# Layer 3's q and k products of both halves of a sample put side by side, and a gate convolution on 128 columns

## The chip, the cores and the metric

The kernel runs on one core of a Trainium2 chip. A core has five engines that run beside each other and meet through semaphores: TensorE (PE, the matrix products; its weight loads are listed as PEld), VectorE (DVE), ScalarE (ACT), GpSimd (POOL) and SyncE (SP, which here issues the transfers). Matrix products write to PSUM, of which this kernel keeps eight banks; the other operands lie in SBUF. The metric is the device time of one execution in microseconds (us): the median of three runs.

## The reference

Four layers are applied in turn to x of 16 samples, 256 channels and 32 x 32 pixels (1024 tokens), in 32-bit floats:

```python
# layer 0: attention of the pixels over one another
xn = group_norm(x, gamma, beta)                 # 8 groups
q, k, v = split(W_qkv xn + b_qkv)
x = x + W_proj(softmax(q k^T / sqrt(256)) v) + b_proj
# layer 1: a gate from two planes of the image
w1, w2 = mean(x, channels), max(x, channels)
w3 = relu(conv3x3([w1, w2]) + b1)
x = x * sigmoid(conv3x3(w1 + w2 + w3) + b2)
# layer 2: attention as in layer 0, with its own norm and weights
# layer 3: attention with 32 channels for q and k, and clipped energies
energy = clip((Wq x + bq)^T (Wk x + bk) / sqrt(32), -10, 10)
x = gamma * (Wv x + bv) softmax(energy)^T + x
```

## The kernel before, in words

The samples are worked on in two streams, called lanes: even samples in one, odd ones in the other. Each lane is a Python generator (`stream`), and one step of it ends at a `yield`; the kernel takes a step of each lane in turn, after a head start of 30 steps (`OFFSET`) for the even lane. The steps and the pauses between them (the `W_` numbers; `wait(n)` gives n empty steps) thus set which work of one sample stands beside which work of the other. A framework then fixes the order of the instructions of each engine when the program is built.

A large matrix product is made with seven block products in the place of eight (`seven`): it takes combined blocks of its left operand (`combine`, L900 to L905, tile xs) and of its right operand, and adds the seven results up in four PSUM banks. The banks' letters are the names in the profile: b, a, c and f, with a prefix. Products of the first attentions' q and k side are tb, ta, tc, tf; of the values (`values`) vb, va, vc, vf, evicted into the tile vt; of the logits (`logits`) sb, sa, sc, sf, evicted into e by ACT copies (L672) and DVE additions (L603), with exponentials on ACT (L682, L684). In `seven` a bank is read by ACT's copy between two products that add into it: sb<-tc must be copied before the next product, sb<-t, adds to the same bank.

`weighted` (L687) makes the product of the exponentials and the values in the same way, on banks b, af and c. Its steps are b(vt), af(tv), af(vt), c(tv), b(tv), c(vt), b(vt), named here by the operand in brackets. DVE makes the combined operands cb (L698) and further ones in e (L699, L746, L751). After c(tv), DVE takes a reciprocal of the row sums (L755) and ACT copies the bank (L756), and then c(vt) adds into it; after c(vt) come L762, additions (L725) and the update of the tokens (L732). All these products are recorded by one helper (`product`, L571), so the profile tells them apart by tile.

`group_norm` (L106) normalizes a sample that comes up: statistics on DVE (L114 to L134), a power on POOL (L138), coefficients on DVE (L141 to L144), and the scaling of one half on DVE (L145) and one on ACT (L146).

`clipped_attend` (L1053) is layer 3. For each half h of the tokens it makes q and k with eight products on 64 columns of the array (L1072: two row-halves of a bank side by side, two channel chunks, four pairs); three ACT evictions (L1084) and three DVE evictions (L1088) lay the bank out in the tile t_qk. After the evictions of the second half, DVE makes the combined blocks (`combine`). The first step of the values stands between the two halves. Then the values go on, and for each half of the queries and each half of the keys a block of eight score products (L1107, tile s, 32 rows of the array), four exponentials on ACT (L1123) and clips on DVE (L1128) follow, then `weighted`.

`gate_of` (L159) is layer 1. Its first convolution is two products (L169) of which only 32 columns of the array are used, with 32-column weights `k.toep[:, i, :]`, and its result stands in 32 partitions of a bank. Its second convolution (L182) uses weights of 128 columns, four copies of one 32-column matrix. `toep` holds six 32-column matrices: two of the first convolution and the four copies.

In the profile a 32-bit product appears as two instructions: a block of eight score products as 16, a group of eight products of `weighted` as 16. Where the same tile name serves several shapes, the timeline tells the shapes.

Of the kernel before, what the change touches and what calls it, by code (L numbers as in the profile page):

```python
# [16 lines left out]
P = 128  # L17
# [5 lines left out]
NH = HW // HALF  # L23
TPH = HALF // P
GROUP = 32
DQK = 32
G4 = P // DQK
PH = P // 2
STRIP = 32
# [122 lines left out]
def neighbours(nc, rows):  # L152

    own, before, after = (rows[i * STRIP : (i + 1) * STRIP] for i in range(3))
    nc.vector.tensor_copy(before[..., 1:], own[..., :-1])
    nc.scalar.copy(after[..., :-1], own[..., 1:])


def gate_of(nc, k, small, psum, ptag, pl, rows, nm):  # L159

    for g in range(NG):
        copy = nc.scalar.copy if g % 2 else nc.vector.tensor_copy
        copy(rows[:STRIP, :2, g * NT : (g + 1) * NT], pl[g * STRIP : (g + 1) * STRIP])
    neighbours(nc, rows[:, :2])
    c1 = psum.tile([P, HALF], FP, tag=ptag, name=f"c1_{nm}")
    for i in range(2):
        nc.tensor.matmul(  # L169
            c1[:STRIP, :STRIP], k.toep[:, i, :], rows[:, i, :], start=(i == 0), stop=(i == 1)  # L170
        )
    r1 = small.tile([STRIP, STRIP], FP, tag="r1", name=f"r1_{nm}")
    nc.vector.tensor_scalar(
        r1, c1[:STRIP, :STRIP], k.sc[:STRIP, S_B1 : S_B1 + 1], 0.0, ALU.add, ALU.max
    )
    yield None
    inner = rows[:STRIP, 2, :]
    nc.vector.tensor_tensor(inner, rows[:STRIP, 0, :], rows[:STRIP, 1, :], ALU.add)
    nc.vector.tensor_tensor(inner, inner, r1, ALU.add)
    neighbours(nc, rows[:, 2])  # L180
    c2 = psum.tile([P, HALF], FP, tag=ptag, name=f"c2_{nm}")
    nc.tensor.matmul(  # L182
        c2[:, :STRIP],
        k.toep[:, 2:, :].rearrange("p g j -> p (g j)"),
        rows[:, 2, :],
        start=True,
        stop=True,
    )
    yield None

    sg = small.tile([P, NT], FP, tag="sg", name=f"sg_{nm}")
    for g in range(NG):
        gs = slice(g * STRIP, (g + 1) * STRIP)
        nc.scalar.activation(
            sg[gs], c2[gs, g * NT : (g + 1) * NT], AF.Exp, bias=k.neg_b2[gs], scale=-1.0
        )
    nc.vector.tensor_scalar(sg, sg, 1.0, None, ALU.add)
    nc.vector.reciprocal(sg, sg)
    yield sg


def fast_path(nc, tc, k, bad, x, w_l0, w_l2, w_l3, qk_bias, v_bias, tap_idx, out):
# [7 lines left out]
    with ExitStack() as ctx:  # L210
# [16 lines left out]
        def bank(nm):  # L227
            return ps_m.tile([P, HALF], FP, tag="m", name=nm)
# [5 lines left out]
        def slot(what, lane, shape, nm):  # L234

            return qkvp.tile(shape, FP, tag=f"{what}_{lane}", name=f"{what}_{nm}", bufs=1)
# [304 lines left out]
        rows = [wts.tile([P, 3, STRIP], FP, name=f"rows{lane}") for lane in range(2)]  # L541
# [240 lines left out]
        def wait(steps):  # L782

            for _ in range(steps):
                yield
# [95 lines left out]
        def right_of(w, sums):  # L881

            return factors(
                [[w[:, kk, j * P : (j + 1) * P] for j in range(CC)] for kk in range(CC)],
                {
                    "t1": sums[:, 0],
                    "t2": sums[:, 1],
                    "t3": w[:, 0, P:],
                    "-t4": sums[:, 2],
                },  # L890
            )

        def left_of(xt, xs):


            blocks = [[xt[:, half(h), c] for c in range(CC)] for h in range(NH)]
            s1, s2, s4 = (xs[:, i] for i in range(3))
            return factors(blocks, {"s1": s1, "s2": s2, "s3": blocks[1][0], "s4": s4})
# [154 lines left out]
        def clipped_attend(xt, y, lane, b):  # L1053

            qk = slot("t", lane, [P, NH, 2, 2 * P], f"qk3_{b}")
            groups = ((1, 0, 0), (0, 1, 1), (0, 0, 0), (1, 1, 0))  # L1060
            vt = vts[lane]
            left = left_of(xt, slot("xs", lane, [P, 3, TPH, P], f"l3_{b}"))
            steps = values(lane, left, right_of(*folded["l3"]), f"l3_{b}")
            qt = TPH // 2
            for h in range(NH):
                ps = bank(f"qk3_{b}_{h}")


                for c in range(CC):
                    for i in reversed(range(2)):  # L1070
                        g0 = h * TPH + i * qt
                        nc.tensor.matmul(  # L1072
                            ps[i * PH : (i + 1) * PH, : qt * P].rearrange(
                                "p (g n) -> p g n", g=qt
                            ),
                            w3qk[:, c, i],
                            xt[:, g0 : g0 + qt, c],
                            start=(c == 0),
                            stop=(c == CC - 1),
                        )  # L1080
                low, high, full = slice(0, PH), slice(PH, P), slice(0, 2 * P)
                g0, g1, g2, g3 = (slice(g * DQK, (g + 1) * DQK) for g in range(G4))
                for to, src, blk in ((low, low, 0), (g2, g0, 0), (g2, g1, 1)):
                    nc.scalar.activation(  # L1084
                        qk[to, h, blk], ps[src, full], AF.Identity, bias=qb[src]
                    )
                for to, src, blk in ((low, high, 1), (g3, g3, 0), (g3, g2, 1)):
                    nc.vector.tensor_scalar(qk[to, h, blk], ps[src, full], qb[src], None, ALU.add)  # L1088

                if h:  # L1090
                    combine(left)
                yield
                if not h:
                    next(steps)
                    yield
            yield from steps
            tv = value_sums(lane)
            yield
            ri = small.tile([P, NT], FP, tag="ri", name=f"ri3_{b}")
            for h in range(NH):  # L1100
                e = expp.tile([P, NT, HALF], FP, tag="e", name=f"e3_{b}_{h}")
                for mh in range(NH):
                    ss = [bank(f"s3_{b}_{h}_{mh}_{g}") for g in range(G4)]
                    for j in range(2):
                        for g, (_, _, blk) in enumerate(groups):
                            gs = slice(g * DQK, (g + 1) * DQK)
                            nc.tensor.matmul(  # L1107
                                ss[g][:, j * 2 * P : (j + 1) * 2 * P].rearrange(
                                    "p (t g j) -> p t g j", t=TPH, g=2
                                ),  # L1110
                                qk[gs, mh, 1 - blk, j * P : (j + 1) * P],
                                qk[gs, h, blk].rearrange("p (g t j) -> p t g j", g=2, t=TPH),
                                start=True,
                                stop=True,
                            )

                    for a in range(2):
                        m = mh * TPH + 2 * a
                        part = e[:, m : m + 2, :]
                        by_strip = part.rearrange("p m (t g n) -> p m t g n", t=TPH, g=2)  # L1120
                        for g, (ka, qa, _) in enumerate(groups):
                            if ka == a:
                                nc.scalar.activation(  # L1123
                                    by_strip[:, :, :, qa],
                                    ss[g].rearrange("p (m t n) -> p m t n", m=2, t=TPH),
                                    AF.Exp,
                                )
                        nc.vector.tensor_scalar(part, part, EXP_MIN, EXP_MAX, ALU.max, ALU.min)  # L1128
                    yield from wait(W_EXP)
                yield from wait(W_AV3)  # L1130
                if b == B - 1 and h == NH - 1:
                    last = combp.tile([P, TPH, C], FP, tag="cb", name="last")
                    yield from weighted(e, vt, tv, y, ri, h, f"l3_{b}", last)
                    store_last(last, b, h)
                    continue
                yield from weighted(e, vt, tv, y, ri, h, f"l3_{b}")
                turn_strips(y, half(h))
                chores[lane].extend(in_pairs(y, half(h), bstrip3))
                chores[lane].append(functools.partial(store_tokens, y, b, h))
                yield  # L1140
            count(ri, f"l3_{b}")
# [59 lines left out]
        ps = bank("badp")  # L1201
# [317 lines left out]
```

## Time and profile before

| what | number |
|---|---|
| runs (us) | 2702.98, 2702.78, 2701.82; median 2702.78 |
| profiled execution, span (us) | 2702.3 |
| mean granted TensorE clock | 0.997 of full speed |
| busy PE / PEld / DVE / ACT / POOL (us) | 2658.2 / 2366.0 / 2153.9 / 1327.9 / 45.4 |
| q and k products of layer 3 (L1072) | 256 instructions on 64 columns, 379 ns each |
| products of the first convolution (L169) | 64 instructions on 32 columns, 196 ns each |
| weight loads: 128, 64 and 32 columns (median) | 191, 136 and 110 ns |
| traffic | 123.07 MB moved, 46 GB/s |

The span is the time from the first to the last instruction of one profiled execution; its own time was not taken apart from it, and the median of the unprofiled runs lies 0.5 us above the span. PE's products are pipelined: an instruction's own duration (275 ns for one of 128 columns moved) is longer than the distance to the next one's start (112 ns in a dense row), so work on PE is counted by starts here: 112 ns for 128 columns moved, about 215 for 256 and 429 for 512. An arrow in a row, `out<-in`, names the tile written and those read; the brackets at the end name the idle time of the engine before the row and who ended it.

### The profile page before, as it was taken

Reading aid. Unit: us, or ns where it says so; the run is one execution under the profiler, and the core shown is the slowest. Engines: PE = TensorE matmul, PEld = TensorE weight load, DVE = VectorE, ACT = ScalarE, POOL = GpSimd, SP = SyncE. Lnnn points to the kernel's source line nnn. Section 1 sums busy time; section 2 is a strip of 40 time slices with the busy share of each in tenths; the row PEclk is TensorE's granted clock in tenths of the full one; section 3 lists DMA queues with packets and bytes.
Section 4 is the critical chain, followed back from the end, with each engine's and each line's share of the span. In section 5 each row is a group of like instructions: output and inputs, shape, how many; then the busy total and the mean of one; then the engine's idle time right before and its main releaser. Section 6 shows DMA issues by size and latency. Waiting matters only on the chain.

```text
span 2702.3 us, 47717 instructions
## 1 busy us (share of the span) xinstructions
PE 2658.2 (98%) x18998; PEld 2366.0 (88%) x18998; DVE 2153.9 (80%) x4242; ACT 1327.9 (49%) x2810; POOL 45.4 (2%) x118
## 2 busy tenths in 40 slices
PE   8999999999999999999999999999999999999997
PEld 6888988888988889889889898988989889898897
DVE  7988886888778887788867888678887788868776
ACT  3454455544455445544455544554454544545443
POOL 1000000000000000000000000000000000000000
PEclk9999999999999999999999999999999999999999
DMA  4021111212111120211201212112111121101111
GB/s 115 1 63 48 56 32 24 63 48 63 25 46 50 42 76 9 55 48 48 63 16 48 63 35 61 32 32 63 48 48 32 32 63 55 40 17 34 52 34 41
DMA packets 134823, 123.07 MB, mean 46 GB/s; under 512 B 10689, under 2 KB 125633, under 8 KB 134593
## 3 DMA queue, kind: packets, MB, share of 16 engines
q1 hardware_dynamic: 132720, 118.63, 15.7%
q8 instruction: 152, 2.49, 0.4%
q10 hardware_dynamic: 1872, 1.31, 0.2%
q14 instruction: 79, 0.64, 0.1%
HBM read 69.58 MB, written 50.33 MB: 44 GB/s over the span
## 4 chain that ended last, share of the span: by engine, by line
PE 81%; DVE 13%; ACT 4%; issue 2%; DMA 1%; POOL 0%; DVEq 0%; SPq 0%; ACTq 0%
PE b_l L571 15%; PE c_l L571 11%; PE af_l L571 11%; PE sb_l L571 10%; PE sc_l L571 8%; PE sf_l L571 4%; PE sa_l L571 3%; PE vb_l L571 3%; PE tb_l L571 3%; PE vc_l L571 2%; PE tc_l L571 2%; PE s L1107 2%; DVE e_l L603 1%; DVE vt L603 1%; PE vf_l L571 1%
## 5 line engine op out<-in xcount | busy, mean ns | idle before, releaser
L672 ACT COPY e_l<-sb_l 128x512 f32<-128x512 f32 x384 | 222.5, 584 | 217.9 <-PE sb_l L571 216.7
L571 PE MATMUL sb_l<-t_l,x 128*128 128x256 f32 x1024 | 262.0, 386 | 0.3
L571 PE MATMUL b_l<-vt,e_l 128*128 128x128 f32 x2048 | 251.8, 275 | 0.0
L571 PEld LDWEIGHTS b_l<-vt,e_l 128*128 128x128 f32 x2048 | 244.2, 192 | 5.4 <-issue 2.3
L571 PEld LDWEIGHTS sb_l<-t_l,x 128*128 128x128 f32 x1024 | 180.5, 191 | 40.1 <-ACT e_l L672 11.2
L682 ACT ACTIVATE e_l<-e_l 128x512 f32<-128x512 f32 x256 | 160.9, 630 | 86.6 <-DVE e_l L603 85.7
L684 ACT ACTIVATE e_l<-e_l 128x1024 f32<-128x1024 f32 x128 | 135.5, 1059 | 118.4 <-DVE e_l L603 118.4
L571 PE MATMUL c_l<-tv,cb_l 128*128 128x129 f32 x1536 | 189.0, 275 | 0.2 <-DVE cb_l L698 0.2
L571 PEld LDWEIGHTS c_l<-tv,cb_l 128*128 128x128 f32 x1536 | 180.3, 191 | 6.9 <-PE qk L1072 3.1
L603 DVE TENSOR_TENSOR e_l<-sc_l,e_l 128x512 f32<-128x512 f32 x128 | 88.0, 687 | 116.6 <-PE sc_l L571 114.9
L925 ACT COPY vt<-vb_l 128x512 f32<-128x512 f32 x144 | 84.5, 587 | 147.2 <-PE vb_l L571 146.1
L487 ACT ACTIVATE xr<-xr,bstrip 128x128 f32<-128x128 f32 (+1 forms) x376 | 134.4, 443 | 44.1 <-DVE xr L494 44.1
L1123 ACT ACTIVATE e<-s 128x512 f32<-128x512 f32 x256 | 131.8, 606 | 22.1 <-PE s L1107 21.4
L756 ACT COPY acc_l<-c_l 128x256 f32<-128x256 f32 x96 | 35.4, 368 | 212.3 <-DVE ri_l L755 151.8
L571 PE MATMUL sc_l<-tc_l,xs_l 128*128 128x256 f32 x512 | 134.0, 384 | 2.3 <-DVE vt L603 2.3
L571 PE MATMUL af_l<-tv,e_l 128*128 128x128 f32 x1024 | 131.6, 278 | 4.3 <-ACT e_l L682 4.3
L571 PE MATMUL sc_l<-t_l,xs_l 128*128 128x256 f32 x512 | 133.0, 382 | 0.8
L571 PE MATMUL sa_l<-t_l,x 128*128 128x256 f32 x512 | 132.4, 381 | 0.0
L571 PE MATMUL sf_l<-tc_l,x 128*128 128x256 f32 x512 | 131.7, 380 | 0.0
L571 PE MATMUL sb_l<-tc_l,xs_l 128*128 128x256 f32 x512 | 131.7, 379 | 0.0
L571 PEld LDWEIGHTS af_l<-tv,e_l 128*128 128x128 f32 x1024 | 121.3, 192 | 10.8 <-ACT e_l L682 7.7
L1128 DVE TENSOR_SCALAR e<-e 128x1024 f32<-128x1024 f32 x128 | 83.0, 687 | 59.0 <-ACT e L1123 59.0
(245 smaller groups left out, 5984.6 us busy)
## 6 DMA issues: line engine op xcount, KB each, us to landing
x<-mid_x SPq DMA_DIRECT2D x64, 512.0 KB, 3.3
xr<-in_x_dram SPq DMA_DIRECT2D x64, 256.0 KB, 4.9
mid_x<-t_z SPq DMA_DIRECT2D x128, 128.0 KB, 2.3
mid_x<-t_l SPq DMA_DIRECT2D x128, 128.0 KB, 2.3
x<-in_x_dram SPq DMA_DIRECT2D x62, 256.0 KB, 4.0
out_dram<-xr SPq DMA_DIRECT2D x124, 128.0 KB, 2.3
raw_l<-in_w_l_dram SPq DMA_DIRECT2D x1, 1024.0 KB, 6.9
raw_l<-in_w_l_dram SPq DMA_DIRECT2D x2, 256.0 KB, 5.5
```

The costliest lines, as they stand in the source:

```text
L487: nc.scalar.activation(y[:, s, ts], y[:, s, ts], AF.Identity, bias=bias[:, s : s + 1])
L571: mm = nc.tensor.matmul(out, left, right, start=fresh and m == 0 and (lone or i == 0), stop=(m == len(pairs) - 1), skip_group_check=True,)
L603: nc.vector.tensor_tensor(dst, src, dst, ALU.add)
L672: nc.scalar.copy(block(i, j), ps.rearrange("p (m n) -> p m n", m=2))
L682: nc.scalar.activation(part, part, AF.Exp)
L684: nc.scalar.activation(e[:, m : m + 2, :], e[:, m : m + 2, :], AF.Exp)
L756: nc.scalar.copy(acc[:, hi, c2], c[:, :, :P])
L925: nc.scalar.copy(block(i, j), ps.rearrange("p (m n) -> p m n", m=TPH))
L1107: nc.tensor.matmul(ss[g][:, j * 2 * P : (j + 1) * 2 * P].rearrange("p (t g j) -> p t g j", t=TPH, g=2), qk[gs, mh, 1 - blk, j * P : (j + 1 ...
L1123: nc.scalar.activation(by_strip[:, :, :, qa], ss[g].rearrange("p (m t n) -> p m t n", m=2, t=TPH), AF.Exp,)
L1128: nc.vector.tensor_scalar(part, part, EXP_MIN, EXP_MAX, ALU.max, ALU.min)
```

## The change

In `gate_of` the first convolution loads 128 columns of weights that begin at its 32-column matrix (the next three matrices ride along) and writes all 128 partitions of its bank. Of the result the same 32 partitions are read as before. In `clipped_attend` the first step of the values goes first and has a `yield` behind it; then the products of both halves follow directly on each other, the second half's first, without a `yield` between them; then the evictions of the first half, `combine`, and the evictions of the second half; then a `yield`. Before there were three yields up to this point, now there are two, so each later step of layer 3 of a sample comes one step earlier beside the other lane.

```diff
@@ gate_of
     c1 = psum.tile([P, HALF], FP, tag=ptag, name=f"c1_{nm}")
+    wide = k.toep.rearrange("p g j -> p (g j)")
     for i in range(2):
         nc.tensor.matmul(
-            c1[:STRIP, :STRIP], k.toep[:, i, :], rows[:, i, :], start=(i == 0), stop=(i == 1)
+            c1[:, :STRIP],
+            wide[:, i * STRIP : i * STRIP + P],
+            rows[:, i, :],
+            start=(i == 0),
+            stop=(i == 1),
         )
@@ clipped_attend
             qt = TPH // 2
-            for h in range(NH):
-                ps = bank(f"qk3_{b}_{h}")
-
-
+            next(steps)
+            yield
+            pss = [bank(f"qk3_{b}_{h}") for h in range(NH)]
+            for h, ps in reversed(list(enumerate(pss))):
                 for c in range(CC):
                     for i in reversed(range(2)):
                         g0 = h * TPH + i * qt
...
-                low, high, full = slice(0, PH), slice(PH, P), slice(0, 2 * P)
-                g0, g1, g2, g3 = (slice(g * DQK, (g + 1) * DQK) for g in range(G4))
+            low, high, full = slice(0, PH), slice(PH, P), slice(0, 2 * P)
+            g0, g1, g2, g3 = (slice(g * DQK, (g + 1) * DQK) for g in range(G4))
+            for h, ps in enumerate(pss):
                 for to, src, blk in ((low, low, 0), (g2, g0, 0), (g2, g1, 1)):
                     nc.scalar.activation(
                         qk[to, h, blk], ps[src, full], AF.Identity, bias=qb[src]
                     )
                 for to, src, blk in ((low, high, 1), (g3, g3, 0), (g3, g2, 1)):
                     nc.vector.tensor_scalar(qk[to, h, blk], ps[src, full], qb[src], None, ALU.add)
-
-                if h:
+                if h == 0:
                     combine(left)
-                yield
-                if not h:
-                    next(steps)
-                    yield
+            yield
             yield from steps
```

## The prediction

> **What bounds the kernel now.** I read the page's busy shares and chain first: TensorE (PE) is busy 98% of the span, and the chain that ended last is 81% PE. So a microsecond counts only where PE stands still or runs slowly. Then the waits of PE, longest first in total: they name every place where it stands.
>
> ```profile
> PE 2658.2 (98%) x18998; PEld 2366.0 (88%) x18998; DVE 2153.9 (80%) x4242; ACT 1327.9 (49%) x2810; POOL 45.4 (2%) x118
> ...
> PE 81%; DVE 13%; ACT 4%; issue 2%; DMA 1%; POOL 0%; DVEq 0%; SPq 0%; ACTq 0%
> ```
>
> ```profile
> PE af_l L571 <- ACT e_l L682: 4.3, 16, 0.3
> ...
> PE c_l L571 <- ACT acc_l L756: 2.4, 9, 0.3
> ...
> PE vc_l L571 <- DVE xs_l L902: 2.3, 1, 2.3
> ```
>
> The waits after set-up are a few tenths each, so there is little to win by removing them; but a step moved in PE's fixed order can make new ones. Both columns of the last three lines (times, longest) are used below. The body repeats every 330 us, one even and one odd sample per period (seven alike, and the last pair different); I work on the period of samples 8 and 9. Last come the timelines of PE, ScalarE (ACT) and VectorE (DVE) at the four places that the change moves. Columns: start, duration, engine, line, work.
>
> **1. The merge of the q and k products.** PE's timeline around one of the 32 blocks of eight products on 64 columns:
>
> ```profile
> 1652.12 1.95 PE L571 MATMUL b_l<-vt,e 128*128 128x128 f32 x16
> 1654.00 1.08 PE L1072 MATMUL qk<-x,w3qk 128*64 128x256 f32 x8
> 1655.01 1.12 PE L571 MATMUL tb_l<-x,m_l 128*128 128x512 f32 x2
> 1655.97 1.02 PE L571 MATMUL ta_l<-x,m_l 128*128 128x512 f32 x2
> ```
>
> The 16 products before take 16 x 0.112 = 1.79 us start to start, so the block's turn begins at 1653.91; the products after start at 1655.01, and the first pair of them needs 1655.97 - 1655.01 = 0.96 instead of 2 x 0.429 = 0.86, thus 0.10 of refill. Together 1.20 us. The eight products run in four pairs, two side by side, one pair each 0.215 us (the pace of a 256-wide product): 0.86. So going in and out of the 64-column form costs about 0.35. The change makes 16 blocks of 32: **-0.35 per sample, 16 x -0.35 = -5.6 us**, all of it on PE and uncovered. If the first pair of the second half were not overlapped this would shrink; bounds 0.25 to 0.45 per sample.
>
> A rule of the Trainium skill bears on it, "TensorEngine Tiling (Array Packing)", Key Properties: a change of tiling mode drains the array. The 0.35 above is the trace's price for it; the page has none.
>
> **2. The gate's first convolution.** 16 blocks of four instructions. An even sample's block stands between two parts of one product, PE's rows:
>
> ```profile
> 2441.02 0.61 PE L571 MATMUL af_l<-tv,e_l 128*128 128x128 f32 x4
> ...
> 2441.56 0.31 PE L169 MATMUL c_l<-rows,toep 128*32 128x32 f32 x4
> ...
> 2442.17 1.49 PE L571 MATMUL af_l<-tv,e_l 128*128 128x128 f32 x11 [0.30 <-ACT e_l L682]
> ```
>
> Its turn starts at 2441.02 + 4 x 0.112 = 2441.47, and the next product at 2442.17 (plus 0.10 refill): 0.80. But the last bracket says that PE then waited for ACT's e (the wait list counts it 16 times, 4.3 us). So a shorter block is paid back by that wait: worth 0. The odd block (2488.26) stands free and costs 0.44. In the full-width form the nearest row is the second convolution, L182, whose instructions start 0.103 to 0.112 apart: 4 x 0.107 = 0.43. **Change 0** for both; bounds -0.3 (the 128-wide steps overlap as the 32-wide do) to +0.3 (not even the loads hide) per gate, +-5 us over all, with 0 the likely value as both forms' rows agree.
>
> A rule speaks against this edit: "TensorE: Matmul & The Clock Gate", LDWEIGHTS, has a weight load cost its columns divided by 1.2 in nanoseconds. By it 128 columns for 32 are an estimate of 80 ns more per load, 64 loads, +5.1 us. The load records (110 ns for 32 columns, 191 for 128) show that step of 81 too, but PE's spacing does not follow them: 128-wide loads lie under 0.112 spacing everywhere. By the rows 0, by the rule +5.
>
> **3. What moves.** The value products' first step now goes ahead, one yield per sample is gone, and with it all later layer-3 work of a lane stands one step earlier among the other lane's work. Instruction counts of PE, DVE and ACT are unchanged, and the orders on the DMA queue (SP) and POOL too. The built program lists the new order; two stretches of it put a product nearer to what it waits for.
>
> *Wait A, even samples.* Before, the exps of the second score block (s, L1107) have two products of the other lane's logits behind them. Now the sequence on PE is s block, sb(tc), sc(t), third sb; on ACT the four exps of that s block, then the copy of sb(tc), on which the third sb (it adds into the same bank) waits. The durations come from the block at 1600.74:
>
> ```profile
> 1600.74 1.15 PE L1107 MATMUL s<-t_qk 32*128 32x256 f32 x16
> 1601.81 1.13 PE L571 MATMUL sc_l<-tc_l,xs_l 128*128 128x256 f32 x4
> 1601.96 2.07 ACT L1123 ACTIVATE e<-s 128x512 f32<-128x512 f32 x4 [1.34 <-PE s L1107]
> ...
> 1603.89 0.62 ACT L672 COPY e_l<-sc_l 128x512 f32<-128x512 f32 x1
> ```
>
> Call the s block's start S. The copy behind the exps ends at 1603.89 + 0.62 - 1600.74 = S + 3.77, and PE goes on 0.06 later: S + 3.83. PE is ready sooner: the next product starts at S + 1.07, has 0.10 of refill, and two groups of 0.865 stand before the third sb: S + 2.90. Wait 0.93, plus 0.10 refill: **+1.0 us**. Queued behind the stopped sb on PE is everything; behind the copy on ACT is only the copy that follows. In return the small waits of the old order (sc 0.16 at 1604.56, c and the s block 0.08) go: -0.24.
>
> *Wait B, even samples.* c(vt) adds into a bank that ACT's copy (L756) must first read; the copy needs DVE's reciprocal, and on ACT it stands behind the next sample's normalization (L146). Before, it was just in time:
>
> ```profile
> 1621.28 1.23 DVE L698 TENSOR_TENSOR cb_l<-e_l 128x1024 f32<-128x1024 f32 x1
> ...
> 1635.08 0.81 DVE L145 TENSOR_SCALAR x<-x,a_l,bb_l 128x1024 f32<-128x1024 f32 x1
> ```
>
> ```profile
> 1635.86 1.25 ACT L146 ACTIVATE x<-x,bb_l,a_l 128x1024 f32<-128x1024 f32 x1
> 1637.21 0.37 ACT L756 COPY acc_l<-c_l 128x256 f32<-128x256 f32 x1
> ```
>
> ```profile
> 1637.63 2.05 PE L571 MATMUL c_l<-vt,e_l 128*128 128x129 f32 x16
> ```
>
> From the end of the third sb (1619.07) to c(vt) PE had 18.6 us of work. In the new order one group of 16 products (1.79, the first c of sample 8) stands ahead of that sb and no longer between the two: 16.8. DVE's chain is not shorter. It starts with cb 2.2 after that sb, and from cb to the norm's coefficients took 1635.08 - 1621.28 = 13.8; in the new order the pause of 0.8 for POOL's power (DVE's idle before 1634.49) is filled by two clips of 0.6 each, and a reciprocal goes ahead too, so 14.2 to 14.4. Then ACT: norm 1.25, copy 0.37. Sum 2.2 + 14.3 + 1.25 + 0.37 + 0.05 = 18.2, against 16.8: **+1.3 us**, with refill about 1.4. It hides behind nothing. Bounds: 0 if the norm's chain starts earlier (DVE has 20% idle), 2.0 if the clips wait for exps. In the last pair there is no next sample to normalize, so no wait B.
>
> *Odd samples.* The logits' sc waits for DVE's vt at 1679.78 with 0.49 + 0.11; one step less cover makes it 0.8: +0.2. *Last pair.* The 2.3 us of vc for xs shrink, since the merge brings the combine on DVE nearer: about -1.2, beside A's +1.0 and the other gains: -0.8 in all.
>
> **Sum.** Per period: -0.70 merge, -0.24, +1.0 A, +1.4 B, +0.2 = **+1.66**; seven: +11.6; last pair -0.8: +10.8. From the profiled span of 2702.3: 2713.1; the median of the runs (2702.78) lies 0.5 above the span: **2714 us, +0.4%**.
>
> **Rivals.** R1: neither wait comes, since the shifted DVE and ACT work is early (for it: DVE is 20% idle, ACT 51%; against: both chains above are serial, with hardly an idle stretch): 16 x (-0.35 - 0.12), -7.5: 2695. R2: only one of A and B is there: A alone +0.26 a period, +1; B alone +0.66, +4: 2701 to 2707, no change to be measured. R3: B grows past 2 us and PE falls to half pace. The trace has one such case, and these rows (stretch, length, PE, PEld, DVE, ACT, POOL, granted clock, DMA) are before and after its 2.28 us pause:
>
> ```profile
> 2640.00:2647.00 7.00, 7.00 (x61) 5.77 (x59) 4.81 (x12) 2.80 (x7) 0.20 (x1) 1.00 0.28 90
> ...
> 2649.40:2652.90 3.50, 3.48 (x19) 3.48 (x20) 3.42 (x6) 1.50 (x3) 0.00 (x0) 0.59 0.57 150
> ```
>
> The clock fell to 0.59 for 3 us, about 1.6 us lost; pauses of 1.2 to 1.9 us at 2661 to 2682 show none. With B at 2.2 and this loss each time: 7 x (0.8 + 1.6) = +17 more, 2730. "TensorE: Matmul & The Clock Gate", Part 1, has the fall come after an idle window of some 3.4 us; here it came after 2.28. By the page R3 needs a longer wait. R4: the gate edit does not do what it says but costs 0.3 each: +5, inside the range.
>
> **Chances.** Both waits (forecast) 0.45; R1 0.13; R2 0.27; R3 0.10; others 0.05. The range 2695 to 2727 reaches R1's time and most of R3. What this kernel's measurement can tell from no change is 0.2%, 5.4 us. Faster (below 2697.4) 0.13; same 0.32 (R2, and the forecast with B at its low bound); slower 0.55.
>
> **What would show it.** In the profile after: 16 blocks of 16 qk instructions, each 0.35 shorter than two old ones; a wait of sb on ACT's copy of about 0.9, 8 times; a wait of c on L756's copy of about 1.3, 7 times; gate blocks at 0.43 (odd) with the af wait longer. I am wrong if the sb and c waits stay at tenths, or if waits turn up elsewhere, above all at s blocks or vb.

## The result, and the profile after

The changed kernel takes 2719.89 us in the median (2718.99 to 2723.19), against 2702.78 (2700.66 to 2703.83) before, five runs each: ratio 1.0062 [1.0051, 1.0073], 17.1 us slower. Here and below the brackets behind a ratio are its 95% interval. The forecast was 2714 in a range of 2695 to 2727: the side and the range were right, the size was short by 6 us. The profiled execution has a span of 2718.1 us (2702.3 before) and a mean granted clock of 0.996 (0.997).

Below, in this order: busy time by engine and the chain that ended last, both from the page after.

```profile
PE 2657.7 (98%) x18998; PEld 2373.3 (87%) x18998; DVE 2151.6 (79%) x4242; ACT 1329.4 (49%) x2810; POOL 55.3 (2%) x118
...
PE 75%; DVE 17%; ACT 5%; issue 2%; DMA 1%; POOL 1%; DVEq 0%; SPq 0%; ACTq 0%
```

The work is the same (the same counts, PE busy 0.5 us less), and the span grew by 15.8: PE stands still more. In the chain 6% of the span went from PE to DVE, ACT and POOL, so there are places where PE now waits for other engines. The waits of PE after name them (us in total, times, longest):

```profile
PE c_l L576 <- ACT acc_l L761: 12.6, 15, 1.9
...
PE sb_l L576 <- ACT e_l L677: 5.7, 9, 0.7
...
PE af_l L576 <- ACT e_l L687: 3.3, 16, 0.2
...
PE vc_l L576 <- DVE xs_l L907: 0.6, 1, 0.6
```

Lines of `product`, `logits` and `weighted` are 5 higher than before (L571 is L576, L756 is L761). The wait of c for ACT's copy rose from 2.4 to 12.6, and that of sb is new: waits B and A of the prediction, where it put them. The wait of vc for xs fell from 2.3 to 0.6.

**The merge**, PE's timeline after (start, duration, engine, line, work):

```profile
1593.62 1.95 PE L1077 MATMUL qk<-x,w3qk 128*64 128x256 f32 x16
1595.50 1.16 PE L576 MATMUL vc_l<-vc_l,xs_l 128*128 128x128 f32 x8
```

One block of 16 where there were two of 8. Counted from start to start, with the refill of the next product, it takes 2.07 us, against two blocks of 1.21: 0.35 less per sample.

**The gate**, PE's timeline after, the block that was shown of before:

```profile
2456.03 0.53 PE L170 MATMUL c_l<-rows,toep 128*128 128x32 f32 x4
2456.74 1.60 PE L576 MATMUL af_l<-tv,e_l 128*128 128x128 f32 x12 [0.18 <-ACT e_l L687]
```

The block takes 0.53 instead of 0.31 and the wait behind it 0.18 instead of 0.30. From its turn to the next product it is 0.81 (0.81 before), and for the odd sample, where no wait stands behind, 0.448 (0.438). In the wait list above, af's waits for e fell from 4.3 to 3.3 in all, as eight even blocks at 0.12 make: what the block takes longer, the wait gives back.

**Wait A**, PE and ACT in the timeline after, an even sample:

```profile
1610.30 1.15 PE L1109 MATMUL s<-t_qk 32*128 32x256 f32 x16
...
1611.46 2.06 ACT L1125 ACTIVATE e<-s 128x512 f32<-128x512 f32 x4 [1.33 <-PE s L1109]
...
1613.39 0.62 ACT L677 COPY e_l<-sb_l 128x512 f32<-128x512 f32 x1
...
1614.06 1.13 PE L576 MATMUL sb_l<-t_l,x 128*128 128x256 f32 x4 [0.69 <-ACT e_l L677]
```

ACT takes its instructions in the program's order: the copy that frees the sb bank starts only as the four exponentials end (at 1611.46 + 2.06 = 1613.52; the records overlap by 0.13), and the sb product starts 0.05 after the copy. That is 3.76 after the score block's start (3.83 in the prediction). PE was free 0.85 earlier; the bracket says 0.69 because PE's records end later than its next start can be. Eight times.

**Wait B**, DVE, ACT and PE in the timeline after, the even sample of the fifth period:

```profile
1645.02 0.16 DVE L760 RECIPROCAL ri_l<-c_l 128x2 f32<-128x2 f32 x1
1645.13 1.24 ACT L146 ACTIVATE x<-x,bb_l,a_l 128x1024 f32<-128x1024 f32 x1 [1.67 <-DVE bb_l L144]
...
1646.28 0.35 ACT L761 COPY acc_l<-c_l 128x256 f32<-128x256 f32 x1
...
1646.68 2.05 PE L576 MATMUL c_l<-vt,e_l 128*128 128x129 f32 x16 [1.47 <-ACT acc_l L761]
```

The reciprocal is done at 1645.18, but the copy of the bank stands behind the next sample's normalization and runs at 1646.28. The seven pauses of this kind last 1.77, 1.70, 1.54, 1.48, 1.64, 2.09 and 1.48 us, 11.7 in all (1.3 each in the prediction).

After the longest of them, in period six, the clock falls. The row is a stretch of the trace after: its length, busy PE, PEld, DVE, ACT and POOL, the granted clock, the DMA share and GB/s.

```profile
1979.00:1982.40 3.40, 3.40 (x21) 3.40 (x22) 1.93 (x3) 2.15 (x5) 0.00 (x0) 0.68 0.07 16
```

Seventeen instructions start about 0.21 apart in the place of 0.11: 1.7 us.

### The profile page after: what moved, and what is told of

Its sections match the earlier page's. It is cut to its first block, busy times and chain, and to the rows that moved or that the text cites. A ratio compares the mean times of both kernels' runs of the same rounds, so it can differ in the third digit from the quotient of the medians.

```text
span 2718.1 us, 47706 instructions
## 1 busy us (share of the span) xinstructions
PE 2657.7 (98%) x18998; PEld 2373.3 (87%) x18998; DVE 2151.6 (79%) x4242; ACT 1329.4 (49%) x2810; POOL 55.3 (2%) x118
## 4 chain that ended last, share of the span: by engine, by line
PE 75%; DVE 17%; ACT 5%; issue 2%; DMA 1%; POOL 1%; DVEq 0%; SPq 0%; ACTq 0%
PE b_l L576 14%; PE c_l L576 11%; PE af_l L576 11%; PE sb_l L576 10%; PE sc_l L576 7%; PE sf_l L576 4%; PE sa_l L576 3%; PE vb_l L576 3%; PE tb_l L576 2%; PE vc_l L576 2%; DVE e_l L608 2%; PE tc_l L576 1%; PE s L1109 1%; DVE xr L737 1%; DVE vt L608 1%
## 5 line engine op out<-in xcount | busy, mean ns | idle before, releaser
L576 PE MATMUL sb_l<-t_l,x 128*128 128x256 f32 x1024 | 264.1, 387 | 6.0 <-ACT e_l L677 5.7
L576 PE MATMUL b_l<-vt,e_l 128*128 128x128 f32 x2048 | 251.8, 275 | 0.0
L576 PEld LDWEIGHTS b_l<-vt,e_l 128*128 128x128 f32 x2048 | 244.2, 192 | 5.4 <-issue 2.3
L576 PEld LDWEIGHTS sb_l<-t_l,x 128*128 128x128 f32 x1024 | 179.8, 190 | 48.7 <-ACT e_l L677 20.3
L576 PE MATMUL c_l<-tv,cb_l 128*128 128x129 f32 x1536 | 187.4, 274 | 0.2 <-DVE cb_l L703 0.2
L576 PEld LDWEIGHTS c_l<-tv,cb_l 128*128 128x128 f32 x1536 | 180.4, 191 | 1.2 <-DVE cb_l L703 0.4
L761 ACT COPY acc_l<-c_l 128x256 f32<-128x256 f32 x96 | 35.4, 368 | 221.5 <-DVE ri_l L760 155.6
L930 ACT COPY vt<-vb_l 128x512 f32<-128x512 f32 x144 | 84.6, 588 | 118.2 <-PE vb_l L576 116.8
L576 PE MATMUL c_l<-vt,e_l 128*128 128x129 f32 x1024 | 127.0, 277 | 12.6 <-ACT acc_l L761 12.6
L576 PEld LDWEIGHTS c_l<-vt,e_l 128*128 128x128 f32 x1024 | 121.7, 192 | 17.0 <-ACT acc_l L761 15.7
L576 PE MATMUL sc_l<-tc_l,xs_l 128*128 128x256 f32 x512 | 133.2, 383 | 2.6 <-DVE vt L608 2.6
L576 PE MATMUL af_l<-tv,e_l 128*128 128x128 f32 x1024 | 130.8, 277 | 3.3 <-ACT e_l L687 3.3
L576 PE MATMUL sc_l<-t_l,xs_l 128*128 128x256 f32 x512 | 132.1, 380 | 0.8
L576 PE MATMUL sb_l<-tc_l,xs_l 128*128 128x256 f32 x512 | 132.5, 381 | 0.0
L576 PE MATMUL sa_l<-t_l,x 128*128 128x256 f32 x512 | 132.4, 381 | 0.0
L576 PE MATMUL sf_l<-tc_l,x 128*128 128x256 f32 x512 | 131.8, 380 | 0.0
```

Of the source, the lines that this page charges most:

```text
L576: mm = nc.tensor.matmul(out, left, right, start=fresh and m == 0 and (lone or i == 0), stop=(m == len(pairs) - 1), skip_group_check=True,)
L761: nc.scalar.copy(acc[:, hi, c2], c[:, :, :P])
L930: nc.scalar.copy(block(i, j), ps.rearrange("p (m n) -> p m n", m=TPH))
```

## The experiments

Each was timed against the kernel before, on the same chip. Two questions were open: does the missing step alone bring A and B, with the merge worth what it was said to be worth; and are A and B caused by what stands ahead on ACT, or by something that goes along with it.

**The gate alone**, on the kernel before:

```diff
-            c1[:STRIP, :STRIP], k.toep[:, i, :], rows[:, i, :], ...
+            c1[:, :STRIP], wide[:, i * STRIP : i * STRIP + P], rows[:, i, :], ...
```

> Only the gate's first convolution is changed (128 columns); layer 3 stays as before. My theory: an even block's gain is paid back by the wait for ACT's e behind it, an odd block costs 0.448 instead of 0.438, so the time is that of before, 2702.8 within 1.5 us. Rival (wider weight loads cost by their columns, 64 x 80 ns): 2708. Rival (leaving the 32-column form saves the 0.35 that a change of form costs at L1072, 16 times): 2697.

Measured: 2703.04 against 2703.41, ratio 1.0 [0.9991, 1.001]. The gate edit is worth nothing that can be measured. In its trace the block takes 0.53 and the wait behind it 0.18, as above. The longer loads are there (192 ns each in the place of 110), but PE's starts hardly show them: an odd block takes 0.01 us more, and an even one gives the difference back in its wait. The second rival, 0.35 saved for each block that leaves the 32-column form, lies outside the interval too. By an estimate from the rule of the Trainium skill that spoke against the edit ("TensorE: Matmul & The Clock Gate", LDWEIGHTS) it would have been 5.1 us slower, outside this interval of +-2.7.

**The missing step alone**, on the kernel before: the products stay apart, and only the number of steps is what the change makes it.

```diff
                 if h:
                     combine(left)
-                yield
                 if not h:
+                    yield
                     next(steps)
                     yield
```

> The kernel before with one yield fewer and nothing else: layer 3's two halves stay apart with the values' first step between them. My theory: it has both waits in full (0.85 for sb, about 1.7 for c) and none of the merge's gain, so it is the changed kernel plus 5.6 us: 2725 (2722 to 2729). Rival (the waits come from the merge): 2703.

Measured: 2728.32, ratio 1.0097 [1.0081, 1.0112]. The waits of PE in this kernel:

```profile
PE c_l L571 <- ACT acc_l L756: 12.4, 15, 1.8
...
PE sb_l L571 <- ACT e_l L672: 5.5, 8, 0.7
```

Both waits, with nearly the totals of the changed kernel (12.6 and 5.7), without a product merged. So the cost of the change is that of its missing step; and the whole change is the cheaper of the two, as it should be: its ratio, 1.0062, with the merge's 16 x 0.35 = 5.6 us added (0.0021), is 1.0083, just inside the interval here.

**The merge with the step given back**, one pause ahead of the rest of the values:

```diff
             yield
+            yield
             yield from steps
```

> The changed kernel with the lost yield put back behind the evictions, so the later steps of layer 3 stand beside the other lane's work as they did before. My theory: both new waits come from the shift by a step, so here the wait of sb on ACT's copy and that of c on L756's copy fall back to a tenth or less, the merge's 16 x 0.35 = 5.6 us stay, and the time is 2697 (2695 to 2699). Rival (the waits come from the two halves' evictions being crowded together): they stay, 2717 to 2720.

Measured: 2702.27 against 2703.41, ratio 1.0 [0.9991, 1.0009]. A and B are gone (sb is not among the waits, c for L761 is 2.0 in eight waits, none over 0.3), but the 5.6 us of the merge did not come. ACT and PE in its timeline at an odd sample:

```profile
1656.64 2.87 ACT L1090 ACTIVATE t_qk<-qk,qb 64x256 f32<-64x256 f32 x6 [0.20 <-PE qk L1077]
1659.53 0.69 ACT L952 ACTIVATE t_l<-tc_l,tb_l 128x512 f32<-128x512 f32 x1
...
1660.27 1.12 PE L576 MATMUL tc_l<-xs_l,m_l 128*128 128x512 f32 x2 [0.46 <-ACT t_l L952]
```

The merge puts the six q and k evictions of a sample in a row on ACT, 2.87 us, and the eviction of the other lane's tc bank stands behind them; the next tc product adds into that bank. This wait is 0.62 by starts, with refill 0.72, seven times: 5.0 of the 5.6 us. My expectation had missed it: it had counted what the merge does on PE, and not what it does to ACT's queue.

**A pause at another place**, between the two query halves:

```diff
             for h in range(NH):
+                if h:
+                    yield
                 e = expp.tile(...)
```

> The changed kernel with the lost yield put back between the two query halves of layer 3, so the first half's steps are shifted and the second half's are not; the built program then has ACT's acc copy ahead of the norm and DVE's reciprocal behind it by one coefficient only. My theory: the sb wait (0.85 + 0.1, 8 times, 7.7 us) stays in full, the c wait falls to 0.3 or less: 2702.8 - 5.6 + 7.7 + 2 = 2707 (2704 to 2709). Rival (one cause for both waits): 2697 or 2720.

Measured: 2724.12, ratio 1.008 [1.0066, 1.0093]: slower than the change itself, and 17 us off what I expected. Wait A stays, as expected. Wait B falls only to 0.93 to 1.38 in six periods and is 1.95 in the first, after which the clock falls; and two waits of the same kind turn up elsewhere. One is layer 3's own c copy, on DVE and PE in its timeline:

```profile
1660.05 1.31 DVE L524 STREAM_TRANSPOSE t_l<-xr 128x512 f32<-128x512 f32 x2
...
1663.33 0.94 PE L576 MATMUL c_l<-vt,e 128*128 128x129 f32 x6 [0.98 <-ACT acc_l L761]
```

There the reciprocal stands behind transposes (L524), and the wait is 1.14 us by starts each time. The other is vb, 0.86 seven times, which waits for vt copies behind four exponentials. The theory "a pause anywhere ahead of B takes B away" fell: a shift by one step pairs every later product with another queue.

**A pause where each lane needs it**: the even lane's ahead of the values' rest, as in the third experiment, and the odd lane's ahead of its first step, so that the merged block and its evictions fall elsewhere.

```diff
+            if lane:
+                yield
             next(steps)
             yield
...
             yield
+            if not lane:
+                yield
             yield from steps
```

> The changed kernel with both lanes back at the old number of steps, but not at the same place: even samples get the lost yield behind the evictions, odd samples get it ahead of the values' first step, so that odd samples' q and k stand beside the next even sample's first layer as in the changed kernel. My theory: even samples lose both new waits as in the run with the yield restored, and odd samples lose the wait of tc on ACT (0.6 + 0.1 us, 7 times) that ate the merge's gain there, so the whole 16 x 0.35 us stays: 2697.5 (2695 to 2700). Rival (the merge's gain is taken back at whatever step the crowded evictions stand): 2702.

Measured: 2698.26 against 2703.37, ratio 0.9982 [0.9973, 0.9991]: faster than both kernels. No sb and no tc wait is in its list, and c is

```profile
PE c_l L576 <- ACT acc_l L761: 2.7, 10, 0.4
```

The first period takes 328.6 (329.3 before), the others 329.2 to 329.6 (329.9 to 330.2): 0.62 less on average, so most of the merge's 0.70 a period is there once hardly anything is paid for it.

**The normalization taken off ACT**, in the changed kernel, for layer 0 only:

```diff
-    nc.scalar.activation(out[:, 1], xt[:, 1], AF.Identity, ...)
+    if nm.startswith("l0"):
+        nc.vector.tensor_scalar(out[:, 1], xt[:, 1], a[:, 1:2], bb[:, 1:2], ALU.mult, ALU.add)
+    else:
+        nc.scalar.activation(out[:, 1], xt[:, 1], AF.Identity, ...)
```

> The changed kernel with the ACT half of layer 0's normalization (L146) made by DVE instead, so that nothing of it stands ahead of ACT's acc copy. My theory: the copy starts right behind DVE's reciprocal (1645.18 in the changed kernel's trace) and not behind the norm (1646.28), so the c wait falls by 1.1 from about 1.65 to about 0.55 in each of seven periods, the sb wait stays at 0.85, and no drop of the clock is left: 2719.9 - 7.7 - 2 = 2710 (2707 to 2714; DVE gets 0.8 us more work per sample). Rival (the c wait is DVE's alone, through the reciprocal): no change, 2720, or more.

Measured: 2708.44, ratio 1.0019 [1.0009, 1.003]. ACT and PE in its timeline, the place of wait B:

```profile
1641.14 0.37 ACT L766 COPY acc_l<-c_l 128x256 f32<-128x256 f32 x1 [1.76 <-DVE ri_l L765]
...
1641.57 1.60 PE L581 MATMUL c_l<-vt,e_l 128*128 128x129 f32 x12 [0.30 <-ACT acc_l L766]
```

The copy now follows the reciprocal at once. The pause falls to 0.44 to 0.49 in six periods (the first is 1.12), while sb stays at 5.5 us. So about 1.2 us of a wait B, in these six, is the normalization that stands ahead on ACT, and the rest is DVE's chain up to the reciprocal.

**Two of the four exponentials taken off ACT**, in the changed kernel, even samples, first query half, second key half (DVE clips the scores in their place):

```diff
+                                if less:
+                                    nc.vector.tensor_scalar(to, src, EXP_MIN, EXP_MAX, ...)
+                                else:
+                                    nc.scalar.activation(to, src, AF.Exp)
```

> The changed kernel, but for even samples' first query half and second key half two of the four exponentials on ACT are left out: DVE clips those energies straight from PSUM, so the attention weights there are not exponentials. My theory: ACT's copy of sb(tc) then stands behind two exps and not four and ends about 0.95 us earlier, so the sb wait falls from 0.85 to 0.15 or less, 8 times, 7 us: 2713 (2710 to 2719, the upper end if the c wait takes over what the sb wait gives back, because DVE has 0.6 us more to do ahead of it). Rival (sb waits for its bank or for DVE, not for the exps): sb wait as before, 2720.

Measured: 2711.91, ratio 1.0035 [1.0023, 1.0047]. ACT and PE in its timeline, the place of wait A:

```profile
1608.74 0.59 ACT L677 COPY e_l<-sb_l 128x512 f32<-128x512 f32 x1
...
1609.41 1.10 PE L576 MATMUL sb_l<-t_l,x 128*128 128x256 f32 x4
```

Now the sb product has no wait, and B is what it was (c for L761: 12.4 us). Together with the run before it, this separates A and B: each goes alone, by what stands ahead of its copy on ACT.

**Wait B made longer**, in the changed kernel: three further copies of the c bank ahead of ACT's copy.

```diff
             nc.vector.reciprocal(ri[:, n1 : n1 + 2], c[:, :, P])
+            if nm.startswith("l2") and int(nm[3:]) % 2 and h:
+                for i in range(3):
+                    extra = work.tile([P, HALF], FP, ...)
+                    nc.scalar.copy(..., c[:, :, :P])
             nc.scalar.copy(acc[:, hi, c2], c[:, :, :P])
```

> The changed kernel with three more ACT copies of the c bank (about 0.33 us each) ahead of the copy for which c(vt) waits, in odd samples' second half of layer 2; their results go nowhere. My theory of the clock: a pause of PE above about 2 us brings the granted clock down, as at 2.09 in one of the seven periods of the changed kernel. Pauses become 2.5 to 3.1, so all seven bring it down: + 7 x 1.0 for the copies and + 6 x 1.8 for the clock, 2738 (2732 to 2742), mean clock below 0.995. Rival (it takes an idle window of some 3.4 us, and the one fall was chance): +7, 2727.

Measured: 2734.1, ratio 1.0121 [1.0103, 1.0138]. The seven pauses are 2.99, 2.55, 2.33, 2.31, 2.47, 2.98 and 2.31; the clock fell after the second, third, fourth and seventh. Two stretches of its trace, right after the seventh (2.31) and the fifth (2.47), columns as above:

```profile
2323.80:2327.20 3.40, 3.40 (x16) 3.40 (x17) 1.95 (x3) 2.13 (x5) 0.00 (x0) 0.51 0.00 0
1656.70:1660.10 3.40, 3.38 (x30) 3.38 (x31) 1.89 (x3) 2.19 (x5) 0.00 (x0) 1.00 0.00 0
```

In the same 3.4 us PE starts 16 instructions at clock 0.51, and 30 at 1.00, after the shorter and the longer pause. Each fall costs 1.72 to 1.75 us. So my theory (all seven) and the rival (none) both fell, and that the time lies in the range that I gave is luck. The length of the pause alone does not decide; the last section has what these traces show instead.

## Why the prediction was right, and where its sizes were off

In the span the forecast was 2713.1 and the measurement 2718.1. Between the even gates of successive samples a period took 329.3 to 330.2 before and 331.4 to 332.0 after (333.75 once): seven are 15.4 us longer where 11.6 were forecast. The last pair came to +1.3 in the place of -0.8, and the part ahead of the first gate to -1.0 (it takes 128.8 to 132.5 in the ten traces). These make the 5.0. Another 1.3 is how I passed from span to run: the profiled execution after lies 1.8 above its span, and I had added 0.5.

- **The merge, -0.35 per sample**: right. The block shows it, and with the pauses placed by lane 4.3 of the 4.9 us that it is worth in seven periods are there in the trace.
- **The gate, 0**: right in size (first experiment). I had the wait behind an even block growing and the block shrinking; it is the other way round, and the sum of both stays at 0.81.
- **Wait A, 0.93 and refill 0.10, eight times**: right; 0.85 and 0.11, and it goes when exponentials ahead of the copy go.
- **Wait B, 1.3, seven times**: right in place and cause (third and sixth experiments), and mis-sized: 1.67 on average. In the two shortest, 1.48, DVE's chain from cb to L145 takes 14.56 in the place of my 14.2 to 14.4. What each of the others has above 1.48 equals, to 0.01, a gap in that chain that my sum did not have: behind cb, DVE's statistics of the next sample start late. Around the sixth pause DVE's timeline has

```profile
1962.26 1.23 DVE L703 TENSOR_TENSOR cb_l<-e_l 128x1024 f32<-128x1024 f32 x1
1964.01 0.69 DVE L114 BATCH_NORM_STATS2 st_l<-x 128x6 f32<-128x512 f32 x1 [0.52 <-DMA x<-in_x_dram]
```

  a gap of 0.6 by starts, the largest of the seven, ahead of the longest pause, 2.09; the gap is zero ahead of the two pauses of 1.48. The bracket names the sample's load, but that the load is the cause of every gap is argued and not shown: no earlier load was tried.
- **The clock (R3)**: taken for 0 in the forecast, and the third rival's mechanism came once in the body: a pause of 2.09, 1.7 us lost (1.6 by the prediction's row).
- **Odd samples, +0.2**: 0.05 (sc's waits for DVE's vt went from 2.3 to 2.6 in all). Why so little was not traced.
- **The small waits of the old order, -0.24 a period**: too large. In the period from the even gate at 1458.60, sc's wait (0.15 with refill) is gone as forecast, but c's stays, and a wait of 0.05 at vb is new: some 0.05 came back.
- **Last pair, -0.8**: the step that failed in sign. The combine did come nearer (vc for xs 2.3 to 0.6) and the old fall of the clock at that place is gone; but a score block now waits 0.8 for DVE's t_qk (L1094) and vc 0.8 for ACT's vt (L930), neither of which I had counted, and the clock falls at another place (0.50 from 2693.6 to 2700.5). These two waits are also there in the two runs that keep the merge and give the steps back, and not where the step alone is missing; so they come with the merge.

Over seven periods, the terms that I measured add 2.6 for B, 1.7 for the clock, -0.5 for A and -1.1 for the odd samples to the forecast: 2.7 of the 3.8 us. The other 1.1, 0.16 a period, is about what the small waits fell short of their -0.24; they were counted in one period only.

R1 (no waits, 2695) and R2 (only one of them) are refuted for the change by its wait list, and R4 (the gate costs 0.3 each) by the first experiment. R1's time was in reach all the same: with pauses placed by lane, the merge gives 2698.

## What to carry to other kernels

Where two streams are interleaved step by step, a `yield` that goes with an edit is an edit of its own: count the steps before and after, and keep them equal or move them on purpose. For each product that adds into a bank which another engine must first read, compare the work that PE has left ahead of it with all that stands ahead of that read on its in-order engine; evictions bunched together by a merge count there too. A pause that repairs one lane can hurt the other, so try it lane by lane.

## What the runs showed of the hardware

A fall of the clock cannot be read from the length of PE's pause alone. Between 250 and 2640 us of these ten traces it fell after pauses of 1.95, 2.09, 2.31 (twice), 2.33 and 2.55, and not after 1.98, 2.06, 2.47, 2.98 and 2.99. A fall there lasts 3.4 us at half pace and costs 1.7.

Where the falls begin shows more. In the run with the longer wait B they begin at 654.72, 989.23, 1323.73 and 2323.84: 98, 98 and 293 times 3.4133 us apart. In each of the ten traces all falls lie on such a grid, each trace with its own offset. Cut a trace into pieces along its grid and add up, by starts, how long PE stands in each piece. The six pieces right ahead of a fall hold 1.95, 1.97, 2.09, 2.31, 2.33 and 2.55 us of standing; of all other pieces between 250 and 2640 us, some 7000, none holds more than 1.91. The pause of 2.99 shows how a long one can pass (columns as above):

```profile
316.80:320.21 3.41, 1.98 (x16) 1.79 (x16) 3.14 (x8) 1.73 (x4) 0.47 (x1) 1.00 0.45 119
320.21:323.62 3.41, 2.02 (x18) 2.02 (x19) 0.56 (x1) 3.41 (x10) 0.00 (x0) 1.00 0.15 40
```

It is split between two pieces, 1.60 and 1.39, and the clock stays at 1.00. The pause of 2.31 before the fall at 2323.84 lies whole in one piece. So what goes along with a fall here is how much of one piece PE stands, 1.95 of 3.41 or more. The margin from 1.91 to 1.95 is narrow, and the rule was read from the traces afterwards: no run moved a pause along the grid. Behind 2640 us some falls follow pieces with less standing, and what those go by stays open.

The Trainium skill, "TensorE: Matmul & The Clock Gate", Part 1, tells of a free-running window of 3.4 us: that agrees with the grid and with the length of a fall. That a whole such window must be idle does not agree with the 1.95.

The power that POOL makes for the normalization takes 0.69 us in most places, and in the seven places of wait B, where DVE's clips (L1130) run beside it, 1.16. That is 3.3 of the 9.9 us by which POOL's busy time rose; most of the rest is at L785 (18.9 us; as L780 12.2 before). Whether this is two engines at one resource was not tested.
